# Two of 32 neighbours taken from an SBUF table by ScalarE and VectorE, and a user stage eight positions wide

## The chip, the core and the metric

The kernel runs on one core of one Trainium2 chip. A core has the engines PE (TensorE, matmuls and transposes), DVE (VectorE), ACT (ScalarE), POOL (GpSimd) and SP (SyncE, which here only issues transfers); each works through its own queue in order, and semaphores order them against each other. SBUF is the on-chip memory of 128 partitions, PSUM the smaller one into which PE writes. The metric is the device time in microseconds of one execution.

## The reference

There are 50001 items. Each has 32 neighbours, an "in" and an "out" vector of 32 numbers, and a history vector of 64. The item stage computes, for every item and for each of the two vectors, a softmax attention over its neighbours:

```python
def _neighbor_attn(E, near_full):
    V = E[near_full]
    scores = jnp.einsum('nd,nkd->nk', E, V) / jnp.sqrt(jnp.float32(GEO_HALF))
    w = jax.nn.softmax(scores, axis=-1)
    return jnp.einsum('nk,nkd->nd', w, V)
```

The user stage takes 16384 users with 100 history items each and one target item. With `h` the history vector of an item beside its two attention results (128 numbers), and `t` the same for the target (its own 64 numbers, and the two results in the other order):

```python
x = h * t[:, None, :]
z = relu(einsum('bld,hd->blh', x, W1) + b1)
scores = einsum('blh,h->bl', z, W2[0])
exp_A = exp(scores) * ((history != target[:, None]) & (history != 0))
attn = exp_A / (sum(exp_A, -1) ** 0.5)[:, None]
s = sum(h * attn[..., None])
pred = sum(s * t, -1) / (norm(s broadcast to t) * norm(t))
return sigmoid(pred)
```

## The kernel before

**Item stage.** The items are padded to 23 iterations of 128 partitions by 17 positions (`NITER`, `P`, `NSUB`), so there are 391 positions of 128 items each. `egeo` in HBM holds the in and out vectors of an item side by side, 64 floats. An iteration loads on SP's queue the neighbour indices `nidx`, the items' own vectors `own` and the history vectors `row` (lines 102 to 106). For a position, POOL issues 32 indirect transfers (line 111), one for each neighbour: each takes the 128 indices of a column and fetches 128 rows of 256 bytes into the tile `v`, of which there are five buffers. Then ACT copies the own vectors into PSUM (`own_ps`, line 118), DVE multiplies (`prod`, line 120), sums to the scores (`sc`, 127), takes the maximum (`top`, 129 and 130), ACT takes the exponentials (`ex`, 134), DVE weights (`wv`, two instructions of line 145), sums (`att`, 152) and scales into `row` (153), and ACT copies the two halves in the other order into `trow` (160). At the end of an iteration SP writes `row` to `table` and `trow` to `ttab`, two tables in HBM (163, 164). At the very start ACT issues the copy of the target vectors into `ttab`, 12.5 MB (91, 92).

**User stage.** 128 blocks of 128 users (`UC`), one user per partition. It begins when the tables are written. POOL fetches the target rows `t` of a block (line 197) and, for each of the 100 history positions, 128 rows of 512 bytes of `table` into `h` (line 233). Four positions make a group (`LG`), with 12 buffers of `h`. PE transposes each position (`hT_ps`, 246), DVE multiplies the group by the transposed target (`xT`, 248) and sums `h` over its features (`hsum`, 249), PE multiplies by W1 (`z_ps`, 255), ACT applies relu (`z`, 257), PE multiplies by W2, a matmul for each position (`score`, 265), and at the end of a block the exponentials, the mask (`keep`, 219 and 220) and two sums follow (271 to 275). The loop issues group s beside the hidden layer of group s-1 and the scores of group s-2. A short last part makes the result.

The order of each queue is found by a scheduler from the loop, in both stages.

Of the kernel before, what the change touches and what calls it, by code (L numbers as in the profile page):

```python
# [9 lines left out]

F32 = mybir.dt.float32
I32 = mybir.dt.int32
AF = mybir.ActivationFunctionType
ALU = mybir.AluOpType
AX = mybir.AxisListType

P = 128
ITEMS = 50001
K = 32
# [10 lines left out]
NSUB = 17  # L30
NITER = -(-ITEMS // (P * NSUB))
ROWS = NITER * P * NSUB

# [7 lines left out]
def kernel(  # L43
# [11 lines left out]
    out: bass.AP,  # L55
):
    nc = tc.nc

    const = ctx.enter_context(tc.tile_pool(name="const", bufs=1))
    dram = ctx.enter_context(tc.tile_pool(name="dram", bufs=1, space=bass.MemoryType.DRAM))  # L60
# [25 lines left out]
    egeo_v = egeo.rearrange("(i p j) d -> i p j d", p=P, j=NSUB)  # L86
    ehist_v = ehist.rearrange("(i p j) d -> i p j d", p=P, j=NSUB)
    table_v = table.rearrange("(i p j) d -> i p j d", p=P, j=NSUB)
    ttab_v = ttab.rearrange("(i p j) d -> i p j d", p=P, j=NSUB)

    nc.scalar.dma_start(ttab[0 : ITEMS - 1, 0:DE], etgt[0 : ITEMS - 1, :])
    nc.scalar.dma_start(ttab[ITEMS - 1 : ITEMS, 0:DE], etgt[ITEMS - 1 : ITEMS, :])
    with (
        tc.tile_pool(name="n_in", bufs=2) as n_in,
        tc.tile_pool(name="n_v", bufs=5) as n_v,
        tc.tile_pool(name="n_p", bufs=2) as n_p,
        tc.tile_pool(name="n_s", bufs=3) as n_s,
        tc.tile_pool(name="n_ps", bufs=2, space=bass.MemoryType.PSUM) as n_ps,
    ):
        for it in range(NITER):  # L100
            nidx = n_in.tile([P, NSUB, K], I32, name="nidx")
            nc.sync.dma_start(nidx, near_v[it])
            own = n_in.tile([P, NSUB, 2 * G], F32, name="own")
            nc.sync.dma_start(own, egeo_v[it])
            row = n_in.tile([P, NSUB, D], F32, name="row")
            nc.sync.dma_start(row[:, :, 0:DE], ehist_v[it])
            trow = n_in.tile([P, NSUB, 2 * G], F32, name="trow")
            for j in range(NSUB):
                v = n_v.tile([P, K, 2, G], F32, name="v")
                for k in range(K):  # L110
                    nc.gpsimd.indirect_dma_start(  # L111
                        out=v[:, k].rearrange("p t d -> p (t d)"),
                        out_offset=None,
                        in_=egeo,
                        in_offset=bass.IndirectOffsetOnAxis(ap=nidx[:, j, k : k + 1], axis=0),
                    )
                own_ps = n_ps.tile([P, 1, 2 * G], F32, name="own_ps")
                nc.scalar.copy(own_ps[:, 0, :], own[:, j, :])  # L118
                prod = n_p.tile([P, K, 2, G], F32, name="prod")
                nc.vector.tensor_tensor(  # L120
                    prod.rearrange("p k t d -> p k (t d)"),
                    v.rearrange("p k t d -> p k (t d)"),
                    own_ps.to_broadcast([P, K, 2 * G]),
                    ALU.mult,
                )
                sc = n_s.tile([P, 2, K], F32, name="sc")
                nc.vector.tensor_reduce(sc.rearrange("p t k -> p k t"), prod, AX.X, ALU.add)  # L127
                top = n_s.tile([P, 2], F32, name="top")
                nc.vector.tensor_reduce(top, sc, AX.X, ALU.max)
                nc.vector.tensor_scalar(top, top, -scale, None, ALU.mult)  # L130
                ex = n_ps.tile([P, 2, K], F32, name="ex")
                tot = n_s.tile([P, 2, 1], F32, name="tot")
                for t in range(2):
                    nc.scalar.activation(  # L134
                        ex[:, t, :],
                        sc[:, t, :],
                        AF.Exp,
                        bias=top[:, t : t + 1],
                        scale=scale,
                        accum_out=tot[:, t, :],  # L140
                    )
                nc.vector.reciprocal(tot, tot)  # L142
                wv = n_p.tile([P, 2, G, K], F32, name="wv")
                for t in range(2):
                    nc.vector.tensor_tensor(  # L145
                        wv[:, t].rearrange("p d k -> p k d"),
                        v[:, :, t, :],
                        ex[:, t, :].rearrange("p (k o) -> p k o", o=1).to_broadcast([P, K, G]),
                        ALU.mult,
                    )  # L150
                att = n_s.tile([P, 2, G], F32, name="att")
                nc.vector.tensor_reduce(att, wv, AX.X, ALU.add)  # L152
                nc.vector.tensor_tensor(  # L153
                    row[:, j, DE:D].rearrange("p (t d) -> p t d", t=2),
                    att,
                    tot.to_broadcast([P, 2, G]),
                    ALU.mult,
                )
                for t in range(2):
                    nc.scalar.copy(  # L160
                        trow[:, j, t * G : (t + 1) * G], row[:, j, D - (t + 1) * G : D - t * G]
                    )
            nc.sync.dma_start(table_v[it], row)
            nc.sync.dma_start(ttab_v[it][:, :, DE:D], trow)


    num = const.tile([P, UC], F32, name="num")
# [8 lines left out]
    with (  # L176
        tc.tile_pool(name="u_in", bufs=2) as u_in,
        tc.tile_pool(name="u_t", bufs=2) as u_t,
        tc.tile_pool(name="u_h", bufs=12) as u_h,
        tc.tile_pool(name="u_x", bufs=3) as u_x,  # L180
        tc.tile_pool(name="u_s", bufs=2) as u_s,
        tc.tile_pool(name="ps_t", bufs=3, space=bass.MemoryType.PSUM) as ps_t,
        tc.tile_pool(name="ps_z", bufs=3, space=bass.MemoryType.PSUM) as ps_z,
        tc.tile_pool(name="ps_s", bufs=2, space=bass.MemoryType.PSUM) as ps_s,
    ):
        users = {}
        hists = {}

        def target_rows(c):

# [36 lines left out]

        def gather(c, g):
            u = users[c]
            h = u_h.tile([P, LG, D], F32, name="h")  # L230
            for q in range(LG):
                l = g * LG + q
                nc.gpsimd.indirect_dma_start(  # L233
                    out=h[:, q, :],
                    out_offset=None,
                    in_=table,
                    in_offset=bass.IndirectOffsetOnAxis(ap=u["hidx"][:, l : l + 1], axis=0),
                )
            u["h", g] = h

        def turn(c, g):
            u = users[c]
            h = u.pop(("h", g))
            hT_ps = ps_t.tile([P, LG, P], F32, name="hT_ps")
            for q in range(LG):
                nc.tensor.transpose(hT_ps[:, q, :], h[:, q, :], ident)  # L246
            xT = u_x.tile([D, LG, P], F32, name="xT")
            nc.vector.tensor_tensor(xT, hT_ps, u["tT"].to_broadcast([D, LG, P]), ALU.mult)  # L248
            nc.vector.tensor_reduce(u["hsum"][:, g * LG : (g + 1) * LG], h, AX.X, ALU.add)  # L249
            u["xT"][g] = xT  # L250

        def hidden(c, g):
            u = users[c]
            z_ps = ps_z.tile([HID, LG, P], F32, name="z_ps")
            nc.tensor.matmul(z_ps, w1T, u["xT"].pop(g), start=True, stop=True)  # L255
            z = u_x.tile([HID, LG, P], F32, name="z")
            nc.scalar.activation(z, z_ps, AF.Relu, bias=b1_sb)  # L257
            u["z"][g] = z

        def scored(c, g):  # L260
            u = users[c]
            z = u["z"].pop(g)
            for q in range(LG):
                l = g * LG + q
                nc.tensor.matmul(  # L265
                    u["score"][:, l : l + 1], z[:, q, :], w2_sb, start=True, stop=True
                )
            if g < NG - 1:
                return
            ea = u_s.tile([P, L], F32, name="ea")  # L270
            nc.scalar.activation(ea, u["score"], AF.Exp)
            nc.vector.tensor_tensor(ea, ea, u["keep"], ALU.mult)
            nc.vector.tensor_reduce(den[:, c : c + 1], ea, AX.X, ALU.add)
            nc.vector.tensor_tensor(ea, ea, u["hsum"], ALU.mult)  # L274
            nc.vector.tensor_reduce(num[:, c : c + 1], ea, AX.X, ALU.add)
            del users[c]

        groups = [(c, g) for c in range(UC) for g in range(NG)]
        target_rows(0)
        for s in range(len(groups) + 2):  # L280
            if s < len(groups):
                c, g = groups[s]
                if g == 0:
                    target_work(c)
                if g == NG // 2 and c + 1 < UC:
                    target_rows(c + 1)
                gather(c, g)
                turn(c, g)
# [92 lines left out]
```

## Time and profile before

| | us |
|---|---|
| median of 3 runs (31815.91 to 31817.13) | 31816.24 |
| profiled execution | 31810.23 |
| its span | 31808.5 |
| POOL busy | 24005.7 |
| PE busy | 15238.9 |
| DVE busy | 8951.2 |
| ACT busy | 2851.2 |
| first gather of the item stage starts at | 9.71 |
| first gather of the user stage starts at | 15649.06 |

The mean granted clock of PE over the span is 0.752 of full speed: 1.0 in the item stage, where PE has nothing to do, and 0.5 in the user stage after its first millisecond.

In the profile, "L111" is line 111 of the kernel. A row of a group gives line, engine, operation, output and inputs, and the count; after the bar the busy time in us and the mean duration in ns of one; after the second bar the time that the engine stood idle just before them, and what ended it. A row of a timeline gives the start and the duration in us, and in brackets the idle time before. "issue" is time in which the engine waited for nothing that the trace shows. A row of one line's instructions gives the shortest, median and longest duration in ns. The digits of the page's part 2 are tenths of busy time in 40 equal slices of the span.

### The profile page before, as it was taken

How to read it: one execution, taken by the hardware profiler on the slowest of the kernel's cores; microseconds unless marked ns; L12 is line 12 of the kernel's file. 1: busy time of each engine (PE TensorE's matmuls, PEld its weight loads, DVE VectorE, ACT ScalarE, POOL GpSimd, SP SyncE). 2: the span in 40 equal slices, each digit the busy share in tenths (PEclk: the TensorE clock that was granted, in tenths of full speed). 3: DMA queues.
4: the chain of work that ended last, by engine and by line, in shares of the span. 5: the costliest groups of instructions: out<-in, count | busy, mean ns of one | idle time of the engine just before them, and what ended most of it. 6: DMA issues, size and time to landing. Idle time of an engine off the chain costs nothing.

```text
span 31808.5 us, 154035 instructions
## 1 busy us (share of the span) xinstructions
PE 15238.9 (48%) x44931; PEld 9632.2 (30%) x44931; DVE 8951.2 (28%) x10957; ACT 2851.2 (9%) x6458; POOL 24005.7 (75%) x25446
## 2 busy tenths in 40 slices
PE   0000000000000000000299999999999999999999
PEld 0000000000000000000155555555555555555555
DVE  2222222222222222222222222222222222222222
ACT  0000000000000000000011111111111111111111
POOL 7777777777777777777777777777777777777777
PEclk9999999999999999999955555555555555555555
DMA  2111111111111111111122222222222222222221
GB/s 50 30 30 30 30 31 33 30 30 30 30 34 30 30 30 30 31 33 28 37 54 53 54 53 54 53 54 54 53 54 53 54 53 54 54 53 54 53 54 52
DMA packets 981064, 1358.75 MB, mean 43 GB/s; under 512 B 559872, under 2 KB 564352, under 8 KB 977280
## 3 DMA queue, kind: packets, MB, share of 16 engines
q0 software_dynamic: 814080, 1258.87, 17.1%
q1 hardware_dynamic: 115952, 77.16, 0.9%
q10 hardware_dynamic: 50192, 12.87, 0.2%
q8 instruction: 363, 5.95, 0.1%
q14 instruction: 477, 3.91, 0.0%
HBM read 1308.76 MB, written 51.30 MB: 43 GB/s over the span
## 4 chain that ended last, share of the span: by engine, by line
POOL 49%; issue 19%; PE 15%; DMA 14%; DVE 2%; ACT 1%; POOLq 0%; ACTq 0%; SPq 0%; DVEq 0%
POOL v L111 35%; POOL h L233 13%; DMA h<-table,hidx 11%; PE z_ps L255 7%; PE score L265 5%; PE hT_ps L246 3%; DMA v<-in_egeo_dram,nidx 2%; DVE xT L248 2%; ACT z L257 1%; POOL t L197 0%; POOLq L233 0%; DVE tT L211 0%; DVE ea L274 0%; DMA nidx<-in_near_dram 0%; DMA ttab<-trow 0%
## 5 line engine op out<-in xcount | busy, mean ns | idle before, releaser
L233 POOL DMA_INDIRECT h<-table,hidx x12800 | 12079.2, 944 | 3900.9 <-issue 3159.2
L111 POOL DMA_INDIRECT v<-in_egeo_dram,nidx x12512 | 11805.1, 943 | 3820.9 <-issue 3719.2
L209 PE MATMUL hT_ps<-ident,t 128*128 128x128 f32 x128 | 53.9, 421 | 15644.7 <-DMA t<-ttab,tidx 15644.7
L265 PEld LDWEIGHTS score<-w_sb,z 128*128 128x128 f32 x25600 | 6225.7, 334 | 1080.8 <-ACT z L257 1074.0
L255 PE MATMUL z_ps<-xT,w1T 128*128 128x512 f32 x6400 | 6526.7, 1123 | 0.0
L265 PE MATMUL score<-w_sb,z 128*128 128x1 f32 x25600 | 5903.9, 335 | 235.4 <-ACT z L257 150.2
L246 PE MATMUL hT_ps<-ident,h 128*128 128x128 f32 x12800 | 4715.0, 439 | 673.3 <-DMA h<-table,hidx 520.3
L249 DVE TENSOR_REDUCE hsum<-h 128x4 f32<-128x512 f32 x3200 | 2194.7, 686 | 9243.7 <-DMA h<-table,hidx 9226.9
L209 PEld LDWEIGHTS hT_ps<-ident,t 128*128 128x128 f32 x128 | 28.8, 225 | 15644.9 <-ACT idf L217 15644.9
L246 PEld LDWEIGHTS hT_ps<-ident,h 128*128 128x128 f32 x12800 | 2676.6, 209 | 5434.3 <-issue 3257.2
L120 DVE TENSOR_TENSOR prod<-v,own_ps 128x2048 f32<-128x2048 f32 x391 | 894.6, 2288 | 10794.7 <-DMA v<-in_egeo_dram,nidx 10794.4
L257 ACT ACTIVATE z<-z_ps,b_sb 128x512 f32<-128x512 f32 x3200 | 2199.1, 687 | 13448.3 <-PE z_ps L255 13335.1
L248 DVE TENSOR_TENSOR xT<-hT_ps,tT 128x512 f32<-128x512 f32 x3200 | 2210.2, 691 | 2028.6 <-PE hT_ps L246 2026.8
L255 PEld LDWEIGHTS z_ps<-xT,w1T 128*128 128x128 f32 x6400 | 1745.4, 332 | 0.0
L145 DVE TENSOR_TENSOR wv<-v,ex 128x1024 f32<-128x1024 f32 x782 | 1398.8, 1867 | 0.0
L118 ACT COPY own_ps<-own 128x64 f32<-128x64 f32 x391 | 84.4, 216 | 11499.9 <-DVE prod L120 11498.4
L127 DVE TENSOR_REDUCE sc<-prod 128x64 f32<-128x2048 f32 x391 | 894.5, 2288 | 13.4
L152 DVE TENSOR_REDUCE att<-wv 128x64 f32<-128x2048 f32 x391 | 893.8, 2286 | 13.4
L160 ACT COPY trow<-row 128x32 f32<-128x32 f32 x782 | 131.7, 215 | 2465.7 <-DVE row L153 2465.7
L134 ACT ACTIVATE ex<-sc,top 128x32 f32<-128x32 f32 x782 | 227.7, 291 | 1081.9 <-DVE top L130 1069.2
L142 DVE RECIPROCAL tot<-tot 128x2 f32<-128x2 f32 x391 | 64.8, 166 | 362.3 <-ACT ex L134 362.3
L197 POOL DMA_INDIRECT t<-ttab,tidx x128 | 120.7, 943 | 60.5 <-issue 60.5
(49 smaller groups left out, 808.6 us busy)
## 6 DMA issues: line engine op xcount, KB each, us to landing
h<-table,hidx POOLq DMA_INDIRECT x12800, 2.5
v<-in_egeo_dram,nidx POOLq DMA_INDIRECT x12512, 2.4
table<-row SPq DMA_DIRECT2D x23, 1088.0 KB, 4.4
own<-in_egeo_dram SPq DMA_DIRECT2D x23, 544.0 KB, 3.6
row<-in_ehist_dram SPq DMA_DIRECT2D x23, 544.0 KB, 6.7
ttab<-trow SPq DMA_DIRECT2D x23, 544.0 KB, 6.8
ttab<-in_etgt_dram ACTq DMA_DIRECT2D x1, 12500.0 KB, 53.5
hidx<-in_history_dram SPq DMA_DIRECT2D x32, 200.0 KB, 2.5
```

The lines of the kernel that those rows point to most:

```text
L111: nc.gpsimd.indirect_dma_start(out=v[:, k].rearrange("p t d -> p (t d)"), out_offset=None, in_=egeo, in_offset=bass.IndirectOffsetOnAxis(a ...
L120: nc.vector.tensor_tensor(prod.rearrange("p k t d -> p k (t d)"), v.rearrange("p k t d -> p k (t d)"), own_ps.to_broadcast([P, K, 2 * G]), ...
L127: nc.vector.tensor_reduce(sc.rearrange("p t k -> p k t"), prod, AX.X, ALU.add)
L145: nc.vector.tensor_tensor(wv[:, t].rearrange("p d k -> p k d"), v[:, :, t, :], ex[:, t, :].rearrange("p (k o) -> p k o", o=1).to_broadcast ...
L152: nc.vector.tensor_reduce(att, wv, AX.X, ALU.add)
L233: nc.gpsimd.indirect_dma_start(out=h[:, q, :], out_offset=None, in_=table, in_offset=bass.IndirectOffsetOnAxis(ap=u["hidx"][:, l : l + 1], ...
L246: nc.tensor.transpose(hT_ps[:, q, :], h[:, q, :], ident)
L248: nc.vector.tensor_tensor(xT, hT_ps, u["tT"].to_broadcast([D, LG, P]), ALU.mult)
L249: nc.vector.tensor_reduce(u["hsum"][:, g * LG : (g + 1) * LG], h, AX.X, ALU.add)
L255: nc.tensor.matmul(z_ps, w1T, u["xT"].pop(g), start=True, stop=True)
L257: nc.scalar.activation(z, z_ps, AF.Relu, bias=b1_sb)
L265: nc.tensor.matmul(u["score"][:, l : l + 1], z[:, q, :], w2_sb, start=True, stop=True)
```

## The change

**Item stage.** A table `geoT` stays in SBUF over the whole kernel: two items' 64 numbers make a column of 128, one number per partition, and 25024 such pairs (`PAIRS`) lie side by side, 4 bytes each per partition, 100 KB. It is made at the start in 66 steps (`transposed`): SP loads up to 384 pairs, PE transposes them in up to three instructions, ACT copies them into the table.

Of a position's 32 neighbours POOL now gathers 30. The last two are taken from the table (`columns`): ACT copies 128 columns, one for each of the 128 items, into a tile `g0`, and DVE 128 columns for the other neighbour into `g1`. Each copy is an instruction of 128 partitions by 4 bytes whose source address is in a register. The registers are loaded 32 at a time from a tile `cols` in SBUF (`registers`), so there are four loads per position on each of the two engines; `cols` is made once for 17 positions by seven small DVE instructions and one PE transpose. PE then turns the two tiles (`turn`), ACT copies the half that belongs to the even item of the pair into `v` (`even`), and DVE overwrites it, where the index is odd, with the other half (`odd_half`, a predicated copy). A third way, by SP, is written out and switched off (`SPNUM` is 0).

The order on PE, ACT, DVE and SP in this stage is now that of the program text. A step `s` issues the gathers and the columns of position s, the turn, products, scores and exponents of s-1, the weighting and sum of s-2, and the end of s-3. The eight parts of `work` have a block of 32 copies of each engine behind every second one. The loads of the next iteration are issued half an iteration ahead, and the two writes of an iteration now stand on ACT's queue. `prod` and `wv` have one buffer instead of two.

**User stage.** A group has eight positions (the last of a block four). `h` has 6 buffers of eight instead of 12 of four; the tiles of PSUM have two buffers instead of three. `xT` and `hsum` are single instructions on eight positions, `hsum` is put behind `xT` and its own waits for the gathers are dropped; the matmul for z and the relu stay at four positions each.

```diff
+AUX = ("AAAA", "DDDD",)
+NAUX = len(AUX)
+SPNUM, SPDEN = 0, 1
+NREG = 32
+PAIRS = ROWS // 2
+NST = 3
...
+    geoT = nc.alloc_sbuf_tensor("geoT", (P, PAIRS), F32).ap()
...
+        tc.manual_schedule(engines={E.PE, E.Activation, E.DVE, E.SP}),
+        tc.tile_pool(name="n_st", bufs=2) as n_st,
         tc.tile_pool(name="n_in", bufs=2) as n_in,
         tc.tile_pool(name="n_v", bufs=5) as n_v,
-        tc.tile_pool(name="n_p", bufs=2) as n_p,
+        tc.tile_pool(name="n_p", bufs=1) as n_p,
+        tc.tile_pool(name="n_g", bufs=2) as n_g,
...
+        def transposed(q):
+            h = min(P, (PAIRS - q * NST * P))
+            n = NST if h == P else 1
+            st = n_st.tile([P, NST, 4 * G], F32, name="st")
+            base = q * NST * P
+            nc.sync.dma_start(
+                st[0:h, 0:n, :],
+                egeo_p[base : base + h * n, :].rearrange("(p n) d -> p n d", n=n),
+            )
+            into = geoT[:, base : base + h * n].rearrange("d (p n) -> d n p", n=n)
+            for n0 in range(0, n, 4):
+                m = min(4, n - n0)
+                ps = n_pt.tile([P, 4, P], F32, name="pt")
+                for r in range(m):
+                    nc.tensor.transpose(ps[:, r, 0:h], st[0:h, n0 + r, :], ident[0:h, 0:h])
...
+                    nc.scalar.copy(into[:, n0 : n0 + m, :], ps[:, 0:m, 0:h])
...
+        def registers(s, a, engine, i0, low, top):
+            it, j = divmod(s, NSUB)
+            r = j * (NAUX + 1) + a
+            _, vals = nc.values_load_multi_w_load_instructions(
+                its[it][5][r : r + 1, i0 : i0 + NREG],
+                engines=[engine],
...
+            for k in range(k1 if by_sp else k1 + 1):
+                nc.gpsimd.indirect_dma_start(
+                    out=v[:, k].rearrange("p t d -> p (t d)"),
...
+        def columns(s, a, i0):
+            e = AUX[a][i0 // NREG]
+            vals = registers(s, a + 1, ENGINE[e], i0, geoT_at, geoT_at + 4 * (PAIRS - 1))
+            g = subs[s]["g"][a].bitcast(U8)
+            copy = nc.scalar.copy if e == "A" else nc.vector.tensor_copy
+            for i in range(i0, i0 + NREG):
+                copy(g[:, 4 * i : 4 * i + 4], geoT_b[:, ds(vals[i - i0] - geoT_at, 4)])
+
+        def turn(s):
+            back = n_pt.tile([P, 4, P], F32, name="pt")
+            for a in range(NAUX):
+                nc.tensor.transpose(back[:, a, :], subs[s]["g"][a], ident)
...
+        def even(s):
+            nc.scalar.copy(subs[s]["aux"], subs[s]["back"][:, 0:NAUX, 0 : 2 * G])
...
+        def odd_half(s):
+            nc.vector.copy_predicated(
...
+            work = [
+                lambda: one and turn(s - 1),
+                lambda: (two and weighted(s - 2, 0), one and even(s - 1)),
+                lambda: two and weighted(s - 2, 1),
+                lambda: one and (odd_half(s - 1), products(s - 1)),
+                lambda: one and scores(s - 1),
+                lambda: two and attend(s - 2),
+                lambda: three and finish(s - 3),
+                lambda: one and exponents(s - 1),
+            ]
+            for w in range(len(work)):
+                work[w]()
+                if s < NT:
+                    for blocks in (acts, dves):
+                        n = len(blocks)
+                        for c in blocks[-(-w * n // 8) : -(-(w + 1) * n // 8)]:
+                            columns(s, *c)
...
-        tc.tile_pool(name="u_h", bufs=12) as u_h,
-        tc.tile_pool(name="u_x", bufs=3) as u_x,
+        tc.tile_pool(name="u_h", bufs=6) as u_h,
+        tc.tile_pool(name="u_x", bufs=2) as u_x,
...
+        LW = 2 * LG
+        NW = -(-L // LW)
...
+            x = nc.vector.tensor_tensor(
+                xT[:, 0:w, :], hT_ps[:, 0:w, :], u["tT"].to_broadcast([D, w, P]), ALU.mult
+            )
+            s = nc.vector.tensor_reduce(
+                u["hsum"][:, g * LW : g * LW + w], h[:, 0:w, :], AX.X, ALU.add
+            )
+            tc.add_manual_dep(s.ins, x.ins.name, in_order, reason="after x")
+            for q in u.pop(("got", g)):
+                tc.declare_no_dep(s.ins, q.ins, reason="after x")
```

## The prediction

> **What bounds the kernel now.** I read the page's parts 1, 2, 4 and 5 first, then the timelines of POOL at the seams of the two stages.
>
> ```profile
> span 31808.5 us, 154035 instructions
> ...
> PE 15238.9 (48%) x44931; PEld 9632.2 (30%) x44931; DVE 8951.2 (28%) x10957; ACT 2851.2 (9%) x6458; POOL 24005.7 (75%) x25446
> ...
> PE   0000000000000000000299999999999999999999
> ...
> POOL 7777777777777777777777777777777777777777
> PEclk9999999999999999999955555555555555555555
> ...
> POOL 49%; issue 19%; PE 15%; DMA 14%; DVE 2%; ACT 1%; POOLq 0%; ACTq 0%; SPq 0%; DVEq 0%
> ...
> L233 POOL DMA_INDIRECT h<-table,hidx x12800 | 12079.2, 944 | 3900.9 <-issue 3159.2
> L111 POOL DMA_INDIRECT v<-in_egeo_dram,nidx x12512 | 11805.1, 943 | 3820.9 <-issue 3719.2
> ```
>
> POOL is 75% busy in every slice: 0.94 us per gather, then 0.30 us in which the trace shows it waiting for nothing. That gap is part of the price: start to start a gather takes 1.248 us in both stages.
>
> ```profile
> 15626.29 0.94 POOL L111 DMA_INDIRECT v<-in_egeo_dram,nidx  x1 [0.30 <-issue]
> 15649.06 0.94 POOL L197 DMA_INDIRECT t<-ttab,tidx  x1 [21.82 <-issue]
> ...
> 31787.64 0.94 POOL L233 DMA_INDIRECT h<-table,hidx  x1 [0.30 <-issue]
> ```
>
> The first gather starts at 9.71 us (timeline of the start). So (15626.29 - 9.71)/12511 = 1.2482 us per neighbour gather and (31787.64 - 15649.06)/12927 = 1.2484 us per user gather: no slack in either. The span is 9.7 + 15616.6 + 22.8 (seam) + 16138.6 + 20.9 (tail) = 31808.6. The profiled execution took 31810.2, the span and 1.7 around it; the median is 31816.2, 6.0 above that. I carry both.
>
> A position of the neighbour stage lasts 32 x 1.248 = 39.9 us, of which DVE works 11.3 and ACT 1.5. In the user stage PE is the second runner:
>
> ```profile
> 16700.00:31000.00 14300.00, 13500.97 (x39805) 8534.85 (x39804) 4061.51 (x6575) 2041.03 (x3289) 10809.18 (x11456) 0.50 0.21 53
> ```
>
> The columns are PE, PEld, DVE, ACT, POOL busy: PE 94% at half clock.
>
> **1. Two gathers less per position.** 391 positions x 2 x 1.2482 = 976 us taken off POOL. It is the whole gain on offer; POOL's budget per position falls to 30 x 1.2482 = 37.4 us, and ACT and DVE must each finish a position within that.
>
> **2. 128 copies per position on ACT and as many on DVE, their addresses from registers.** Copies go out back to back, so what counts is the step between starts, not the duration:
>
> ```profile
> 8005.78 0.17 DVE L142 RECIPROCAL tot<-tot 128x2 f32<-128x2 f32 x1 [0.93 <-ACT ex L134]
> 8005.86 3.58 DVE L145 TENSOR_TENSOR wv<-v,ex 128x1024 f32<-128x1024 f32 x2
> ...
> 8012.06 0.34 ACT L160 COPY trow<-row 128x32 f32<-128x32 f32 x2 [6.30 <-DVE row L153]
> ...
> L130 DVE TENSOR_SCALAR top<-top x391: 168/170/245, 60.7 to 15633.7; 128x2 f32<-128x2 f32 x196
> ```
>
> ACT: two 215 ns copies fill 0.34 us, a step of 0.125; 128 make 16.0 us. If nothing overlaps, 128 x 0.215 = 27.5. DVE: L145 starts 0.08 us after L142, which lasts 0.17; 128 x 0.082 = 10.5 us. Without overlap, by the mean of L130 (0.187), 23.9. I take the overlapped values, since nothing waits between the copies; what a register address adds no row shows, so the upper ends stay for the range.
>
> **3. Four loads of 32 registers per position and engine.** No row of before is such a load, and it holds its engine's queue: the 32 copies behind it need its registers. The floor is about nothing. [...] The nearest row is a sequencer's own wait instruction (L120, DVEq EVENT_SEMAPHORE, median 50 ns). These loads read SBUF, so I take 50 ns a register: 6.4 us, an estimate.
>
> Sum per position. DVE: prod 2.32, sc 2.32, top 0.25 and 0.19, tot 0.08, wv 3.6, att 2.32, row 0.23, the new predicated copy 0.28 (as L211, 128x128 from PSUM), index preparation 0.1 = 11.7; + 10.5 + 6.4 = 28.6 us. ACT: ex 0.88, trow 0.34, own 0.22, the new 128x128 copy 0.27, two writes' issue spread over 17 positions 0.1 = 1.8; + 16.0 + 6.4 = 24.2 us. Both under 37.4: hidden behind POOL. [...] The break-even on DVE is (37.4 - 11.7 - 10.5)/128 = 119 ns a register.
>
> **4. Order.** ACT's even copy of position s-1 waits for its gathers, then products, scores, and the weighting one position later; the column blocks of s stand between. Behind the wait on ACT stand its column blocks 2 to 4 (the DVE's turn and PE's turn wait for those), all with one position of room. v has five buffers and is freed two positions later, so POOL stays at most some three ahead: enough in the steady state. The index preparation of the next 17 positions waits on DVE for nidx, with all DVE work behind it; SP may issue that load when the buffer's last gather is done, some eight positions (300 us) ahead, for a landing of 2.7.
>
> **5. Start.** Before the first column the table of pairs is transposed: 66 steps (SP load, 3 PE transposes, one ACT copy) through two buffers.
>
> ```profile
> 1.39 50.72 ACTq L92 DMA_DIRECT2D ttab<-in_etgt_dram  x1
> ...
> 54.23 0.68 SPq L106 DMA_DIRECT2D row<-in_ehist_dram  x1
> ```
>
> SP's third load sits till 54 us behind the 12.5 MB copy; the new loads stand behind it. A step is a landing (2.7 us for the 272 KB of nidx), an issue (0.44) and PE (0.9), halved by two buffers: 2.0 to 2.5 us with own's 3.6; 2.2 x 66 = 145, ready at 200 us. POOL meanwhile fills its five buffers till 9.7 + 150 x 1.248 = 197 and waits for v of position 0, freed after two positions and the first weightings: 200 + 57 + 5 = 262. A stall of 65 us (40 to 100), once.
>
> **6. Seam and tail.** After the last gather come even 0.5, odd 0.3 and the previous position's attend (2.6) in front of the last exponents: +2.5. The last user group leaves slightly more undone: +2.5. The two DMA writes of an iteration move from SP to ACT; cost in item 3's sum.
>
> **7. The user stage eight wide.** The same 12928 gathers, transposes, z and score matmuls, as wide a h reserve (6 x 8 for 12 x 4); DVE's 691 ns at 512 columns becomes about 1.22 us at 1024, half as often. POOL covers it: nothing. If PE's 5.6% slack is lost (0.55 us per eight positions), each further 0.1 us per eight costs 0.1 x 1600 = 160 us; if PE waits less, nothing is gained, for POOL sets the step.
>
> Sum: -976 + 65 + 5 = -906; span 30902, profiled 30904, median **30910** us.
>
> [...] L219, a one-input SBUF to SBUF operation, took 204 ns in the median and 435 once, and there the gather step was 1.44 us instead of 1.25:
>
> ```profile
> 15651.55 0.94 POOL L233 DMA_INDIRECT h<-table,hidx  x1 [0.30 <-issue]
> 15652.99 0.95 POOL L233 DMA_INDIRECT h<-table,hidx  x1 [0.50 <-issue]
> ```
>
> [...] But 391 runs of L130 left POOL's median and mean at 944 and 943 ns and were themselves stretched by 17 ns in the mean. By that row POOL loses nothing. I take nothing; the gain is gone at (976 - 70)/11730 = 77 ns a gather.
>
> **Rivals.** (A) as summed, 30910; own range 30840 to 31100. (B) part of the gain lost: contention of 15 to 70 ns a gather, or an engine 0.5 to 2 us over 37.4: 31100 to 31750. For it: the upper ends of item 2 give DVE 42. (C) slower: register loads make DVE the bound, from 119 ns a register on; then the whole start counts, for the stage ends at 200 + 391 x the position. [...] At 130 ns (38.8): 15371, 31570, still a gain; it is slower from 39.4 us a position, 135 ns a register. [...] (E) the change doesn't do what it says, POOL still issuing 32: the edit removes both gathers from its loop, no chance worth counting; the user half doing nothing is in A.
>
> **Numbers.** A 0.45, B 0.17, same 0.03, C 0.21, D 0.14. 0.2% is about what a measurement of this kernel tells from no change. Faster 0.62, same 0.03, slower 0.35. Below 30830 lies 0.03, above 33200 (most of C's upper half) 0.14: 30830 to 33200.
>
> **What would show it.** POOL's v row x11730 with a step still at 1.248; one wait of 40 to 100 us before position 5; DVE and ACT idle until gathers. [...]

## The result

The changed kernel takes 30865.35 us (median of 4 runs, 30863.64 to 30865.47) where the kernel before takes 31816.08 (4 runs, 31815.83 to 31817.13): 0.9701 of its time, with an interval of 0.9689 to 0.9713, or 951 us less. The forecast was 30910 us, faster.

The page of the changed kernel, parts 1, 2, 4 and 5:

```profile
span 30863.6 us, 246685 instructions
...
PE 13340.6 (43%) x45932; PEld 7630.5 (25%) x45932; DVE 12128.8 (39%) x58485; ACT 7843.2 (25%) x56963; POOL 23284.3 (75%) x24664
...
PE   0000000000000000000778778877877877887787
...
POOL 7777777777777777777777777777777777777777
PEclk9999999999999999999665666666566566656656
...
POOL 56%; issue 23%; DMA 12%; PE 7%; DVE 1%; another core or an unknown queue 0%; ACT 0%; POOLq 0%; SPq 0%; ACTq 0%; DVEq 0%
...
L438 POOL DMA_INDIRECT h<-table,hidx x12800 | 12084.6, 944 | 3899.7 <-issue 3451.0
L215 POOL DMA_INDIRECT v<-in_egeo_dram,nidx x11730 | 11078.2, 944 | 3599.4 <-issue 3484.2
```

POOL still sets both stages: 75% busy in every slice, 944 ns for a gather, and the idle time before the neighbour gathers is "issue" but for 115 us. The number of neighbour gathers fell from 12512 to 11730. ACT and DVE carry what went: DVE went from 28% to 39%, ACT from 9% to 25%, and neither shows in the chain that ended last with more than 1%.

The timelines of POOL at the start, where it was stalled once, at the seam of the stages and at the end:

```profile
8.57 1.10 POOL L215 DMA_INDIRECT v<-in_egeo_dram,nidx  x1 [7.26 <-DMA nidx<-in_near_dram]
214.75 0.94 POOL L215 DMA_INDIRECT v<-in_egeo_dram,nidx  x1 [18.97 <-DVE wv L294]
...
14677.94 0.94 POOL L215 DMA_INDIRECT v<-in_egeo_dram,nidx  x1 [0.30 <-DMA v<-in_egeo_dram,nidx]
14702.36 0.94 POOL L400 DMA_INDIRECT t<-ttab,tidx  x1 [23.48 <-issue]
...
30845.25 0.95 POOL L438 DMA_INDIRECT h<-table,hidx  x1 [0.30 <-issue]
```

With these the span can be laid out beside that of before:

| us | before | after | difference |
|---|---|---|---|
| until the first gather | 9.71 | 8.57 | -1.1 |
| first to last neighbour gather | 15616.58 | 14669.37 | -947.2 |
| seam | 22.77 | 24.42 | +1.6 |
| first to last user gather | 16138.58 | 16142.89 | +4.3 |
| tail | 20.86 | 18.35 | -2.5 |
| span | 31808.5 | 30863.6 | -944.9 |

The 947.2 are 782 gathers less at 1.2482 us (976.1), 21.2 us of waits longer than a step (18.97 of them the one at 214.75), and 7.7 us because an ordinary step took 1.2489 us in this execution where it took 1.2482 in that of before. The order of the other engines' queues changed with the gathers and was not tried alone; with the whole difference laid to gathers, waits and step, nothing is left for it.

### The profile page after: what moved, and what is told of

Read it like the earlier page. It is cut to its first block, busy times and chain, and to the rows that moved or that the text cites. A ratio compares the mean times of both kernels' runs of the same rounds, so it can differ in the third digit from the quotient of the medians.

```text
span 30863.6 us, 246685 instructions
## 1 busy us (share of the span) xinstructions
PE 13340.6 (43%) x45932; PEld 7630.5 (25%) x45932; DVE 12128.8 (39%) x58485; ACT 7843.2 (25%) x56963; POOL 23284.3 (75%) x24664
## 3 DMA queue, kind: packets, MB, share of 16 engines
q0 software_dynamic: 789056, 1233.20, 17.1%
## 4 chain that ended last, share of the span: by engine, by line
POOL 56%; issue 23%; DMA 12%; PE 7%; DVE 1%; another core or an unknown queue 0%; ACT 0%; POOLq 0%; SPq 0%; ACTq 0%; DVEq 0%
POOL v L215 33%; POOL h L438 23%; DMA h<-table,hidx 10%; PE z_ps L473 3%; DMA v<-in_egeo_dram,nidx 2%; PE score L482 2%; PE hT_ps L453 2%; DVE xT L455 1%; DVE hsum L458 0%; DMA st<-in_egeo_dram 0%; PE pt L180 0%; POOL t L400 0%; POOLq L438 0%; ACT g L229 0%
## 5 line engine op out<-in xcount | busy, mean ns | idle before, releaser
L215 POOL DMA_INDIRECT v<-in_egeo_dram,nidx x11730 | 11078.2, 944 | 3599.4 <-issue 3484.2
L453 PE MATMUL hT_ps<-ident,h 128*128 128x128 f32 x12800 | 5070.5, 414 | 3207.2 <-DMA h<-table,hidx 3025.5
L455 DVE TENSOR_TENSOR xT<-hT_ps,tT 128x1024 f32<-128x1024 f32 (+1 forms) x1664 | 1968.4, 1183 | 10942.7 <-PE hT_ps L453 10942.5
L234 PE MATMUL pt<-ident,g 128*128 128x128 f32 x782 | 363.9, 471 | 13297.0 <-DVE g L229 8118.8
L473 PE MATMUL z_ps<-xT,w1T 128*128 128x512 f32 x6400 | 5799.9, 1007 | 26.6 <-DVE xT L455 26.3
L229 ACT COPY g<-geoT 128x4 uint8 x50048 | 4919.0, 189 | 2153.7 <-issue 2152.4
L229 DVE COPY g<-geoT 128x4 uint8 x50048 | 3885.9, 194 | 2268.1 <-issue 2149.5
L482 PEld LDWEIGHTS score<-w_sb,z 128*128 128x128 f32 x25600 | 4330.9, 255 | 0.6 <-issue 0.5
L482 PE MATMUL score<-w_sb,z 128*128 128x1 f32 x25600 | 4022.1, 279 | 0.1
L458 DVE TENSOR_REDUCE hsum<-h 128x8 f32<-128x1024 f32 (+1 forms) x1664 | 1942.6, 1167 | 0.0
```

Of the source, the lines that this page charges most:

```text
L215: nc.gpsimd.indirect_dma_start(out=v[:, k].rearrange("p t d -> p (t d)"), out_offset=None, in_=egeo, in_offset=bass.IndirectOffsetOnAxis(a ...
L229: copy(g[:, 4 * i : 4 * i + 4], geoT_b[:, ds(vals[i - i0] - geoT_at, 4)])
L455: x = nc.vector.tensor_tensor(xT[:, 0:w, :], hT_ps[:, 0:w, :], u["tT"].to_broadcast([D, w, P]), ALU.mult)
L458: s = nc.vector.tensor_reduce(u["hsum"][:, g * LW : g * LW + w], h[:, 0:w, :], AX.X, ALU.add)
L473: nc.tensor.matmul(z_ps, w1T, xT[:, q : q + LG, :], start=True, stop=True)
L482: nc.tensor.matmul(u["score"][:, l : l + 1], z[:, q, :], w2_sb, start=True, stop=True)
```

## The experiments

The theory: POOL's issue of gathers bounds both stages, so each gather taken away is worth its whole step of 1.248 us, until ACT or DVE needs longer for a position than POOL. (The bytes that a gather fetches do not set the step: in the kernel before it is 1.2482 us with rows of 256 bytes and 1.2484 with rows of 512.) Its rivals: the wide user stage has a part in the gain; the register loads or the copies come near to being the bound; the copies slow POOL down.

### Each half of the change alone

The first kernel has the new item stage with the user stage of before (12 buffers of four positions), the second the item stage of before with the wide user stage. The core of the edit, in the first against the changed kernel:

```diff
-        tc.tile_pool(name="u_h", bufs=6) as u_h,
-        tc.tile_pool(name="u_x", bufs=2) as u_x,
+        tc.tile_pool(name="u_h", bufs=12) as u_h,
+        tc.tile_pool(name="u_x", bufs=3) as u_x,
...
-            hT_ps = ps_t.tile([P, LW, P], F32, name="hT_ps")
-            for q in range(w):
+            hT_ps = ps_t.tile([P, LG, P], F32, name="hT_ps")
+            for q in range(LG):
```

> The new item stage with the user stage of before. Theory (POOL paces both stages, the eight-wide user stage is worth nothing): 30860 to 30870 us, within 0.1% of the changed kernel, all of the gain of 951 us; PE's granted clock in the user stage back at 0.50 and PE back at 94% busy there. Rival (the user half carries a part of the gain, because PE at 94% delayed some gathers): some 100 us or more slower than the changed kernel.

> The user stage eight wide with the item stage of before. Theory: 31816 us, within 20 us of before; the user gathers keep a step of 1.248 us, PE at about 78% busy with a granted clock of about 0.62, as in the changed kernel. Rival (the wide user stage helps): 100 us or more faster than before.

Measured: the new item stage alone 30859.96 us, ratio 0.9702 (0.9685 to 0.9718); the wide user stage alone 31807.68, ratio 1.0 (0.999 to 1.0009). The kernel before took 31808.22 beside them. So the item stage holds the whole gain, and the user stage is worth nothing that can be measured.

The wide user stage does change something. A stretch of it in the changed kernel, and the same stretch with the user stage of before behind the new item stage (columns: PE, PEld, DVE, ACT, POOL busy, PE's granted clock, DMA share, GB/s):

```profile
16000.00:30000.00 14000.00, 11238.20 (x38962) 6491.76 (x38962) 3441.83 (x3774) 1999.97 (x3219) 10584.42 (x11212) 0.62 0.20 53
```

```profile
16000.00:30000.00 14000.00, 13236.90 (x38945) 8347.33 (x38945) 3974.62 (x6436) 1996.31 (x3218) 10585.68 (x11207) 0.53 0.19 53
```

PE does the same 39000 matmuls in 80% of the time instead of 95%, at a granted clock of 0.62 instead of 0.53, and POOL's column is the same within 0.02%. PE was second, not first: what it gains is idle time.

### Which of the two engines copies

```diff
-AUX = ("AAAA", "DDDD",)
+AUX = ("AAAA", "AAAA",)
```

> Both columns of a position are copied by ACT, none by DVE. Theory: ACT needs 2.0 + 8 blocks of 4.07 us (load and 32 copies, as the timeline of the changed kernel shows) = 34.6 us per position, under POOL's 37.4, so the time stays at 30855 to 30870 us, and the step between item gathers falls from 1.2489 to 1.2482 us, that of before (7 us in all), since no DVE copy is beside them. Rival (ACT's blocks don't overlap with its other work and waits): over 37.4 us per position, and 391 us more for each us over.

Measured: 30877.42 us (one run), 12 above the changed kernel and 7 above the expected range. ACT now makes all 256 copies of a position and still keeps up. What it costs is the start, which the expectation had left out, as the timeline shows (the wait was 18.97 us in the changed kernel):

```profile
239.40 0.94 POOL L215 DMA_INDIRECT v<-in_egeo_dram,nidx  x1 [43.23 <-DVE wv L294]
```

That is 24 us more; 12 of them come back, for the ordinary step was 1.2482 us among the neighbour gathers, as expected, and shorter among the user gathers too.

The other way, with both neighbours on DVE:

```diff
-AUX = ("AAAA", "DDDD",)
+AUX = ("DDDD", "DDDD",)
```

> Both columns of a position are copied by DVE, none by ACT. Theory (an engine over POOL's 37.4 us becomes the bound, as in rival C): DVE needs 11.7 + 8 blocks of 3.7 us = 41.3 us per position; the item stage ends at about 172 + 391 x 41.3 = 16320 us, the total is about 32510, slower than before; POOL stands in wait of DVE in each position, and a gather itself stays at 944 ns. [...]

Measured: 31643.96 us (one run), a little faster than before where slower was expected. DVE is the bound, as expected, but at a lower price: a position takes 39.1 us in the mean, not 41.3. The groups of POOL and of the copies, and the timeline of one position on DVE:

```profile
L215 POOL DMA_INDIRECT v<-in_egeo_dram,nidx x11730 | 11069.1, 944 | 4282.6 <-issue 3351.5 <-DVE wv L294 816.7 <-DMA v<-in_egeo_dram,nidx 107.3
L229 DVE COPY g<-geoT 128x4 uint8 x100096 | 7791.7, 195 | 3444.1 <-issue 3319.7 <-ACT geoT L184 117.3
```

```profile
7999.13 2.29 DVE L258 TENSOR_TENSOR prod<-v,own_ps 128x2048 f32<-128x2048 f32 x1
8001.36 2.65 DVE L229 COPY g<-geoT 128x4 uint8 x32
8003.74 2.27 DVE L268 TENSOR_REDUCE sc<-prod 128x64 f32<-128x2048 f32 x1
...
8015.48 2.44 DVE L229 COPY g<-geoT 128x4 uint8 x32 [2.01 <-issue]
8019.30 2.42 DVE L229 COPY g<-geoT 128x4 uint8 x32 [1.39 <-issue]
...
8037.79 2.29 DVE L258 TENSOR_TENSOR prod<-v,own_ps 128x2048 f32<-128x2048 f32 x1
```

From one `prod` to the next 38.66 us, with POOL waiting for `wv` once per position. A block of 32 copies takes 2.42 us or so, 76 ns a copy. The load ahead of it shows as idle time, and only in part: 2.0 us behind a short instruction, 1.39 behind another block, nothing at all behind the 2.3 us of `prod`. The five idle stretches of this position add up to 8.2 us for eight loads of 2.14 us (17.1 us). So 1.0 us of a load shows. My expectation had charged 3.7 us for a block with its load, 1.3 us above the copies, and 11.7 us for the other work, of which some 10.6 show; that is why it came out too long.

This run also settles what the copies do to POOL. 256 copies per position on DVE, twice what the change makes, left a gather at 943.7 ns in the mean (943.5 before) and the step between gathers that did not wait at 1.2484 us.

An effect is there all the same, on the other side. In the changed kernel the same copy takes ACT the same time always, and DVE not (shortest, median, longest in ns):

```profile
L229 DVE COPY g<-geoT x50048: 145/159/427, 171.9 to 14659.8; 128x4 uint8 x200
L229 ACT COPY g<-geoT x50048: 187/189/198, 174.0 to 14636.4; 128x4 uint8 x200
```

A fifth of DVE's copies take over 215 ns, and 96% of these end within 60 ns of the end of a gather on POOL. Of those that start 0.6 to 0.7 us into a gather nearly all are long, 307 ns in the mean; of those that start in its first half microsecond none is over 205. So DVE's copies are held for the last part of each gather and let go with it. It costs DVE little, since the copies behind go on starting: 73 ns from start to start in the mean, 71 in the median. What holds them no run shows.

### Half as many registers in a load

```diff
-AUX = ("AAAA", "DDDD",)
+AUX = ("AAAAAAAA", "DDDDDDDD",)
...
-NREG = 32
+NREG = 16
```

> The changed kernel with 16 registers a load and eight loads per position and engine instead of four of 32. The time stays at 30865 us within 30, since both engines have room. The load's duration tells: if it is paid by the register (50 ns, as in the prediction), a load falls from 1.98 us on ACT and 2.14 on DVE to about half, 1.0 to 1.1; if it is one round trip, it stays near 2.

Measured: 30858.05 us (one run), so the time does not tell 16 from 32: POOL covers both. The loads do. One-line view of the loads (shortest, median, longest in ns), first in the changed kernel with 32 registers, then with 16:

```profile
L189 DVEq TENSOR_LOAD <-cols x1564: 2097/2144/2361, 55.8 to 14655.3; - x196
L189 ACTq TENSOR_LOAD <-cols x1564: 1948/1978/5590, 171.7 to 14631.3; - x196
```

```profile
L189 DVEq TENSOR_LOAD <-cols x3128: 1093/1119/1346, 56.3 to 14654.9; - x196
L189 ACTq TENSOR_LOAD <-cols x3128: 1002/1028/3799, 172.4 to 14647.0; - x196
```

By these two lengths a register costs (2144 - 1119)/16 = 64 ns on DVE and (1978 - 1028)/16 = 59 ns on ACT, and a load some 0.08 to 0.1 us beside that. What is seen of it on ACT is in the group of the copies, again 32 and then 16 registers to a load:

```profile
L229 ACT COPY g<-geoT 128x4 uint8 x50048 | 4919.0, 189 | 2153.7 <-issue 2152.4
L229 DVE COPY g<-geoT 128x4 uint8 x50048 | 3885.9, 194 | 2268.1 <-issue 2149.5
```

```profile
L229 ACT COPY g<-geoT 128x4 uint8 x50048 | 5056.4, 189 | 694.4 <-issue 667.5
```

2153.7/1564 = 1.38 us of idle time per load of 1.98, against 694.4/3128 = 0.22 per load of 1.03. ACT's idle time before the copies falls to a third. A load runs while copies issued earlier are still at work, so that some 0.6 to 0.8 us of it in the mean is hidden, whatever its length: in the trace ACT is busy during 0.75 us of a load of 32 and 0.86 us of one of 16.

### More than two neighbours

If POOL is the bound and the others have room, a third neighbour should be worth as much as the first two. Three neighbours, seven blocks of 32 copies on ACT and five on DVE:

```diff
-AUX = ("AAAA", "DDDD",)
+AUX = ("AAAA", "AAAD", "DDDD",)
```

> Three of 32 neighbours from the table, seven blocks of 32 copies per position on ACT and five on DVE; POOL gathers 29. Theory (the gathers not issued are the whole gain, as long as each engine's position stays below POOL's): POOL 29 x 1.2484 = 36.2 us, ACT 2.0 + 7 x 4.14 = 31, DVE 11.7 + 5 x 3.5 = 29; 391 x 1.2484 = 488 us less than the changed kernel, and some 30 us more of stall at the start, for two slower positions must pass before v is free: about 30405 us. [...]

Measured: 30398.63 us (30396.71 to 30399.36), ratio 0.9557 (0.9541 to 0.9573): 467 us less than with two, for 391 x 1.2482 = 488 us of gathers. The rest is the start, where the one wait grew from 19 to 48 us:

```profile
L215 POOL DMA_INDIRECT v<-in_egeo_dram,nidx x11339 | 10703.6, 944 | 3511.9 <-issue 3357.8 <-DMA v<-in_egeo_dram,nidx 96.9 <-DVE v L247 48.4
```

Next, four neighbours in even positions and three in odd ones (the pool of small tiles goes from three buffers to two to make room):

```diff
-AUX = ("AAAA", "DDDD",)
+AUX = ("AADD", "AAAA", "AAAD", "DDDD")
+HALF = 2
...
-        tc.tile_pool(name="n_s", bufs=3) as n_s,
+        tc.tile_pool(name="n_s", bufs=2) as n_s,
...
+        def first(s):
+            return s % HALF
...
-            for k in range(k1 if by_sp else k1 + 1):
+            for k in range(K - NAUX + first(s)):
```

> Four of 32 neighbours from the table at even positions (nine blocks on ACT, seven on DVE), three at odd ones (seven and five); the small tiles have two buffers instead of three, for SBUF is full. Theory: POOL 28.5 x 1.2484 = 35.6 us per position, ACT 2.0 + 8 x 4.14 = 35.1, DVE 11.7 + 6 x 3.5 = 32.7, so POOL still sets the step, by a little; the stall at the start grows by 40 us: about 30175 us. If waits between the engines cost ACT 1 us more per position, it is 30500.

Measured: 30165.02 us (30163.95 to 30165.34), ratio 0.9483 (0.9468 to 0.9499), the gather's mean still 944 ns:

```profile
L219 POOL DMA_INDIRECT v<-in_egeo_dram,nidx x11143 | 10519.0, 944 | 3462.3 <-issue 3284.7 <-DMA v<-in_egeo_dram,nidx 96.6 <-DVE wv L298 60.5
```

And four in every position, nine blocks on ACT and seven on DVE:

```diff
-AUX = ("AAAA", "DDDD",)
+AUX = ("AAAA", "AAAA", "ADDD", "DDDD",)
...
-        tc.tile_pool(name="n_s", bufs=3) as n_s,
+        tc.tile_pool(name="n_s", bufs=2) as n_s,
```

> Four of 32 neighbours from the table at every position, nine blocks on ACT and seven on DVE; the small tiles have two buffers instead of three. Theory: POOL needs only 28 x 1.2484 = 35.0 us, but ACT 2.0 + 9 x 4.14 = 39.3, so ACT sets the stage: 172 + 391 x 39.3 = 15540 us, total about 31720, slower than with two or three neighbours, and POOL waits for v at every position. Rival (the loads overlap further): below 31000.

Measured: 31706.72 us (one run). The gain is gone at once. The group of POOL, and its timeline where it waits once in every position:

```profile
L215 POOL DMA_INDIRECT v<-in_egeo_dram,nidx x10948 | 10333.0, 944 | 5070.9 <-issue 3112.9 <-DVE wv L294 1842.5 <-DMA v<-in_egeo_dram,nidx 107.6
```

```profile
8025.89 0.94 POOL L215 DMA_INDIRECT v<-in_egeo_dram,nidx  x1 [4.17 <-DVE wv L294]
...
8065.10 0.94 POOL L215 DMA_INDIRECT v<-in_egeo_dram,nidx  x1 [4.53 <-DVE wv L294]
```

A position lasts 39.2 us where POOL needs 28 x 1.248 = 34.9. ACT is at its end, with nine blocks of some 4.07 us and some 2 us of other work in a position, and no idle time but the part of the loads that shows, as its own timeline tells:

```profile
8037.23 3.14 ACT L229 COPY g<-geoT 128x4 uint8 x32 [0.93 <-issue]
8041.28 3.14 ACT L229 COPY g<-geoT 128x4 uint8 x32 [0.91 <-issue]
```

This is the boundary that the prediction was about, met by adding work rather than by the change itself.

By the runs with 16 registers, shorter loads should make room on ACT and bring the version with four back under POOL:

```diff
-AUX = ("AAAA", "DDDD",)
+AUX = ("AAAAAAAA", "AAAAAAAA", "AADDDDDD", "DDDDDDDD")
...
-NREG = 32
+NREG = 16
...
-        tc.tile_pool(name="n_s", bufs=3) as n_s,
+        tc.tile_pool(name="n_s", bufs=2) as n_s,
```

> Four of 32 neighbours at every position with 16 registers a load: of the 32 blocks of 16 copies 18 on ACT and 14 on DVE; two buffers of the small tiles. From the run with 16 registers at two neighbours: on ACT a block of 16 takes (5056 + 694)/3128 = 1.84 us with its load, 3.68 for 32 copies instead of 4.14, since a load of 1.03 us is nearly covered by copies still queued. Theory: ACT 2.3 + 18 x 1.84 = 35.4 us, DVE 11.7 + 14 x 1.7 = 35.5, POOL 28 x 1.2484 = 35.0; the stage ends at 172 + 391 x 35.5 = 14050 us, total about 30230, against 31707 with loads of 32. Rival (the loads' place does not matter, their sum does): 39 us per position as with loads of 32, about 31700.

The first two runs can't be used for that: on the chip on which they stood the kernel before itself took 36135 us. There this version took 44726.23 us, ratio 1.238 (1.2359 to 1.24), and the second time 44705.07, ratio 1.2369 (1.2348 to 1.239).

> The same kernel as four16, whose first run stood on a chip where the kernel before itself took 36135 us, so that it could not be compared. Four of the 32 neighbours are read as columns, with sixteen registers to a load, and 18 blocks of 16 columns on ScalarE beside 14 on VectorE. If the copying engines are the only thing that bounds the version with four (31707 us), a position now costs ScalarE 18 x 1.03 of loads at most and 288 copies of 0.098 = 28.2 us plus its other work, some 35 us in all where part of the loads hides, and VectorE about 35.5 us, both under or near the 34.95 us of 28 gathers: 195.5 pairs of positions at 70 to 72 us give an item stage of 13700 to 14080 us and 29850 to 30250 us in all. If the loads do not hide at all, ScalarE stands at 7.2 + 18.5 + 28.2 = 53.9 us less what it has free, and the time is 31700 us or more, as with the 32-register loads.

> Once more the kernel with four neighbours and sixteen registers to a load; in its first two runs the kernel before itself took 36135 us beside it, 13.6% over its time elsewhere. If that lengthening belongs to the chip of those runs and not to the kernels, the kernel before takes some 31810 us beside this run on another chip, and this version 29850 to 30250 us where the copying engines alone bound the version with four, or 31700 us and more where the register loads do not hide. If the kernel before takes 36135 us again, the reading is again not to be compared with the others, and what sixteen-register loads do for four neighbours stays open.

On another chip, with the kernel before at 31808.46 us, it took 30119.06 (30114.68 to 30125.36), ratio 0.9469 (0.9453 to 0.9485):

```profile
L215 POOL DMA_INDIRECT v<-in_egeo_dram,nidx x10948 | 10350.0, 945 | 3487.2 <-issue 3198.2
L229 ACT COPY g<-geoT 128x4 uint8 x112608 | 11367.7, 189 | 765.1 <-issue 682.3
```

The same 112608 copies with loads of half the length: ACT's idle time before them is 765 us where it was 3748, and POOL's idle time falls from 5071 to 3487. The time falls by 1588 us for a change of one constant and its blocks. It is not told apart from the version with three and a half neighbours, whose interval overlaps.

POOL is not quite the bound again. One more gather less than with three would have been worth 488 us, down to some 29910, and 208 of them are missing. POOL waits for `wv` in many positions (one row of its timeline), and these are the waits of DVE and of ACT between 2000 and 13000 us (total in us, times, longest; a shorter row of ACT, its own loads, is left out):

```profile
8064.60 0.94 POOL L215 DMA_INDIRECT v<-in_egeo_dram,nidx  x1 [2.77 <-DVE wv L294]
```

```profile
DVE g L229 <- issue: 1860.5, 3400, 3.5
ACT v L240 <- PE pt L234: 853.7, 310, 5.2
```

DVE waits for its loads and hardly for another engine (10 us in all for PE); ACT waits for PE's turn, which waits for DVE's copies in nearly every position. So now DVE is full: its position lasts 35.2 us in the mean, where POOL's gathers need 34.9. POOL waits 189 us for `wv` before 153 gathers (53.5 of them once, at the start), and at the seam 120 us, where the changed kernel has 23, until the engines behind it have caught up.

The five divisions of the work in one table (POOL's need is the number of gathers by 1.248):

| neighbours as columns | POOL needs per position, us | measured time, us | who sets the item stage |
|---|---|---|---|
| 2 | 37.4 | 30865 | POOL |
| 3 | 36.2 | 30399 | POOL |
| 3.5 | 35.6 | 30165 | POOL |
| 4, 16 registers | 34.9 | 30119 | DVE, by 0.3 us a position |
| 4, 32 registers | 34.9 | 31707 | ACT |

## Why the prediction was right

It was 45 us too high, 5% of the gain. Its steps:

**Two gathers less (step 1): right.** The forecast of 976 us is 976.1 in the trace, since the step of a gather stayed where it was. Doing the same once more (three) and half as much again (three and a half) was worth what the step says.

**The copies (step 2): the overlapped values were the right ends.** I took 125 ns a copy on ACT and 82 on DVE; the timeline shows 3.14/32 = 98 ns and 2.46/32 = 77 ns:

```profile
8001.63 3.14 ACT L229 COPY g<-geoT 128x4 uint8 x32 [0.94 <-issue]
8018.54 2.46 DVE L229 COPY g<-geoT 128x4 uint8 x32 [2.14 <-issue]
```

A register as an address does not show in it: both are under what I took from instructions with fixed addresses. The upper end (duration by count) would have put DVE over POOL's budget, so the sign of the forecast hung on this choice.

**The register loads (step 3): right in side, low in size.** No run shows a register at 50 ns: that was an estimate from an event instruction, which happened to lie near the 59 and 64 ns measured: luck, not a reading. Both prices are well under the 119 ns from which rival C began. The second error went the other way: the sum charged every load in full, where 0.6 us and more of each is hidden. With the shorter copies, ACT's position needs less than the 24.2 us of the sum (four blocks of 4.07 us and some 2 us of other work are 18.3), and DVE's 26.2 instead of 28.6, read in the first positions, where DVE waits for nothing but its loads:

```profile
217.06 2.29 DVE L258 TENSOR_TENSOR prod<-v,own_ps 128x2048 f32<-128x2048 f32 x1
...
243.29 2.29 DVE L258 TENSOR_TENSOR prod<-v,own_ps 128x2048 f32<-128x2048 f32 x1
```

Both were under 37.4 in any case, so neither error reached the time.

**Order (step 4): right.** In the steady state DVE sits idle ahead of `prod` for 10.83 us, until the gathers have landed, and the stretch repeats after 37.66 us:

```profile
8011.33 2.29 DVE L258 TENSOR_TENSOR prod<-v,own_ps 128x2048 f32<-128x2048 f32 x1 [10.83 <-DMA v<-in_egeo_dram,nidx]
```

**Start (step 5): right in mechanism, the term that was mis-sized.** 65 us were forecast, 40 to 100; the wait was 18.97 us, outside that range. Two terms of it were too long. A step of the table took 1.72 us, not 2.2, for the loads land in 2.4 us and overlap more than two buffers suggested to me; the first copy stands at 171.9 us, not 200. From there to the release of the first `v` it took 43 us, not 62, for each of the two positions in it took some 21 us, not 28.6: the weighting and the sums of earlier positions were not there yet. Together 47 us, nearly the whole error of the forecast. The version with all copies on ACT moved this same wait to 43.23, which fits: it depends on how long the copying engines take for the first positions.

**Seam and tail (step 6)** came to -2 with the beginning, where +5 was forecast: the seam grew by 1.6, and the tail, which was to grow, shrank by 2.5. **The user stage (step 7)** is worth nothing, as forecast, and shown by its run alone; `xT` takes 1225 ns on eight positions, where 1.22 us was estimated.

The rest is small. The ordinary step of this execution was 1.2489 and 1.2488 us in the two stages, where before had 1.2482 and 1.2484: 12 us. The version without copies on DVE had 1.2482 again, but that the copies caused it is not shown, for the user stage has none, and the version with twice as many on DVE had 1.2484. Some short waits in the item stage make 2 us. And I had carried over 6.0 us from the profiled execution to the median, which here is 0: the median stands 1.75 us above the span. In all -46 (start) + 2 + 12 - 7 - 6 = -45.

**The rivals.** D's share of 0.14 was for gathers lengthened by more than 77 ns; that, and the contention in B, fall with the run that put all copies on DVE: a gather took 943.7 ns there and 943.5 before. No run shows the 33200 us at which the forecast's range ends; where another engine set the item stage the runs took 31644 us (DVE, all copies) and 31707 (ACT, four neighbours). The late engine in B falls with DVE's 10.83 us of idle time ahead of `prod`. The longest mean gather is that of the version with four neighbours and 16 registers, 1.8 ns above the one of its user stage (945.4 against 943.6), where 77 would have eaten the gain. What the traces show is DVE's side, copies held to the end of a gather; the 17 ns by which the prediction saw L130 stretched may be of the same kind. C exists, as the versions with all copies on DVE and with four neighbours show, but the change stands 11 us a position away from it (DVE 26.2 against POOL's 37.4).

## What to carry to other kernels

Where one engine's issue of transfers sets the time, price an item of its work by the step from start to start, and move items to engines that idle until the next one's sum per round meets it; here the best was not at two neighbours of 32 but at three and a half or four, 1640 to 1690 us below the kernel before. Before moving them count three things for the receiving engine: the step of its instructions in a row (98 ns a copy on ACT and 77 on DVE here) and not their duration (189 and 194), the register loads (59 and 64 ns a register), and how much of a load the instructions ahead of it cover (0.6 us and more on ACT). Shorter loads, more often, were worth 1588 us where the engine was full and nothing that can be measured where it was not (30858 us for 30865).

## What the runs showed of the hardware that was not expected

- A load of half as many registers from SBUF takes little more than half as long: 2.14 and 1.12 us on DVE for 32 and 16 registers, 1.98 and 1.03 on ACT, and instructions issued before it go on meanwhile, for 0.75 us of a load of 32 on ACT.
- Copies of 4 bytes per partition on DVE are held to the end of POOL's gather when they start in its last 0.4 us (up to 427 ns where the median is 159), and the gather is not lengthened; ACT's are not held (198 ns at most).
- PE with the same matmuls was busy for 80% instead of 95% and was granted a clock of 0.62 instead of 0.53, by the wide user stage alone. Whether it is the order of transposes and matmuls or the width of the groups was not tried.
- On one chip the kernel before took 36135 us, 13.6% more than elsewhere, and the version with four neighbours and 16 registers 48% more. Its trace has gathers as long as ever (943 ns), but in stretches ACT gets its copies out only at multiples of about 0.7 us, and then 114 in one go:

```profile
12031.50 0.19 ACT L229 COPY g<-geoT 128x4 uint8 x1 [1.21 <-issue]
12032.90 0.19 ACT L229 COPY g<-geoT 128x4 uint8 x1 [1.20 <-issue]
12033.60 0.19 ACT L229 COPY g<-geoT 128x4 uint8 x1 [0.51 <-issue]
12034.31 11.54 ACT L229 COPY g<-geoT 128x4 uint8 x114 [0.52 <-issue]
```

DVE keeps the same beat: in the first run there its single copies start at 12014.20, 12015.60 and 12017.00 us, and so do ACT's. The transfers that bring instructions are no more there: 2042 packets on their larger queue, 0.1% of the 16 DMA engines' span, as against 2042 and 0.2% of a shorter span on the other chip. Nothing in the trace says what holds the two engines; the cause stays open. The version with four neighbours has many more small instructions than the kernel before and was hurt more; that this is the reason was not tried.
